# Where the maximum of quantised attention scores is joined, and who copies the transposed words

## The chip, the cores and the metric

The kernel runs on one core of a Trainium2 chip. The metric is the device time of one execution in microseconds; for the kernel before it is the median of three runs. A further execution was profiled, and everything that is read from views of the profile comes from that one. Five engines of the core appear: TensorE (PE, with its weight loads as PEld), VectorE (DVE), ScalarE (ACT), GpSimd (POOL) and SyncE (SP), which only issues transfers here. Each engine works through its own list of instructions in order, and semaphores make one engine wait for another.

## The reference

The reference is a two-layer decoder over 2048 rows of 256 values: sparse and local attention, cross attention and an FFN, then windowed attention, cross attention over image and text, and a mixture of experts, each followed by a layer norm. The change lies in the first cross attention. Its keys, queries and values are rounded to 8 bits, and so are the softmax weights, unsigned, row by row:

```python
attn = jnp.einsum('bhqd,bhkd->bhqk', q, k)
attn = jax.nn.softmax(attn.astype(jnp.float32), axis=-1)
attn = _fq_unsigned(attn, axis=-1)       # s = max(x) / 255; q = clip(round(x / s), 0, 255) * s
out = jnp.einsum('bhqk,bhkd->bhqd', attn, v)
```

There are 16 heads of 16 dimensions, and every query meets all 2048 keys. The largest weight of a row is exp(0) over the sum, so `round(x / s)` is the rounded value of exp(score - max + ln 255): the kernel needs, for each query and head, the maximum over 2048 scores before it can take the exponential.

## The kernel before

The joint stage computes this cross attention and, woven into it, the FFN that follows. Its work is cut into 128 steps: 8 pairs of row blocks (`gp`), 8 pairs of heads (`i`), and the two row blocks of a pair (`u`). One step handles 128 query rows and two heads (`hh`), that is two score rows of 2048 keys for each query. A step has two halves (`part`), and a half has two score blocks of 512 keys for both heads, so four blocks ("quarters") in a step. The loop at the end of the listing writes the order of every engine's instructions out by hand: `later` and `due` put small operations of the FFN, the query preparation and the layer norm into set half-steps.

What happens to one step, over several turns of the loop:

- TensorE computes a block of scores into PSUM (`scores`, L788). There are two such buffers (`s`).
- VectorE scales the block by the query's step and writes it to SBUF as `e` (`scaled`, L795). The same instruction puts the block's maximum into `smx`. In the kernel before, quarters 1 to 3 start from the maximum of the quarter before, which they read as a per-partition operand, so that the fourth column holds the maximum of the row so far. The first quarter has `None` there. In the profile each of these is TENSOR_SCALAR_CACHE_REDUCE with a DVE_READ_ACCUMULATOR behind it.
- ScalarE turns the maximum into ln 255 - max (`exponent`, L810, tile `snl`), at the end of the step.
- One turn later ScalarE takes the exponential of 2048 scores at a time to unsigned bytes (`weights8`, L819), once in each half.
- TensorE transposes these as words of four bytes (`words_T`, L831) into one of two PSUM buffers. The words are copied to SBUF (`words_out`, L837, tile `at`, three buffers): in the first half of a turn by VectorE, in the second by ScalarE.
- GpSimd spreads the bytes of the words to bfloat16 (`spread`, L841, tile `aT`), one cast of 2048 elements in each half.
- TensorE multiplies by the values (`context`, L854).

In a turn of the loop, VectorE's list holds the half's four scalings, then additions and other small work that is due, then the words of the first half. ScalarE's holds small copies that are due first, then the exponential, the words of the second half, the FFN's gate functions (L940, L941), and at the end of the second half `exponent`. GpSimd's holds the cast, then the FFN's elementwise work (L944, L947, L948), query rounding (L618 to L628) and norms; in the first 16 steps it also adds a bias to one row block a step (L1121). FFN work goes to eight of every 16 steps (`units`), from the second pair of row blocks on.

Of the kernel before, what the change touches and what calls it, by code (L numbers as in the profile page):

```python
# [18 lines left out]
F32 = mybir.dt.float32  # L19
# [3 lines left out]
AF = mybir.ActivationFunctionType  # L23
ALU = mybir.AluOpType
AX = mybir.AxisListType
PSUM = bass.MemoryType.PSUM

P = 128
# [20 lines left out]
def decoder(ctx: ExitStack, tc: tile.TileContext, w: dict, out: bass.AP):  # L49
    nc = tc.nc  # L50

    const = ctx.enter_context(tc.tile_pool(name="const", bufs=1))
    stat = ctx.enter_context(tc.tile_pool(name="stat", bufs=4))
# [156 lines left out]
    with ExitStack() as ph:  # L210
        pool = ph.enter_context(tc.tile_pool(name="l0a", bufs=1))
# [12 lines left out]
        wts, bias = {}, {}  # L224
# [297 lines left out]
        states, cks = {}, {}  # L522
# [66 lines left out]
    with ExitStack() as ph:  # L589
        pool = ph.enter_context(tc.tile_pool(name="l0x", bufs=1))  # L590
# [172 lines left out]
        nc.sync.dma_start(out=wp2, in_=w["L0_xattn_Wp"].rearrange("(c p) n -> p c n", p=P))  # L763
        for c in range(2):
            nc.gpsimd.tensor_scalar(wp2[:, c], wp2[:, c], sv[:, c : c + 1], 1.0, ALU.mult, ALU.mult)
        ln255 = pool.tile([P, 1], F32, name="ln255")
        nc.gpsimd.memset(ln255, math.log(255.0))

        wk = ph.enter_context(tc.tile_pool(name="l0x_k", bufs=2))
        ps = ph.enter_context(tc.tile_pool(name="l0x_ps", bufs=1, space=PSUM))  # L770
# [20 lines left out]
        def scaled(gp, i, u, half, c, st, s):  # L791

            quarter = 2 * half + c
            for hh in range(2):
                nc.vector.tensor_scalar(  # L795
                    st["e"][hh][:, half, c * G : (c + 1) * G],
                    s[:, hh, :],
                    qs[2 * gp + u][:, 2 * i + hh : 2 * i + hh + 1],
                    None if quarter == 0 else st["mx"][:, quarter - 1, hh : hh + 1],
                    ALU.mult,  # L800
                    ALU.max,
                    accum_out=st["mx"][:, quarter, hh : hh + 1],
                )
# [2 lines left out]
            return 4 * (i // 2) + i % 2 + 2 * hh  # L806

        def exponent(st):
            st["nm"] = stat.tile([P, 2], F32, tag="snl", name="snl")
            nc.scalar.activation(st["nm"], st["mx"][:, 3, :], AF.Identity, bias=ln255, scale=-1.0)  # L810

        def weights8(gp, i, u, hh, st):

# [20 lines left out]
        def words_out(hh, st, pt, copy):  # L834

            at = wk.tile([P, 4, P], F32, tag="at", name="at", bufs=3)
            copy(at.bitcast(U16), pt.bitcast(U16))  # L837
            st["at"][hh] = at
# [126 lines left out]
        states, aTs, os = {}, {}, {}  # L965
# [10 lines left out]
        def due(at, engine):  # L976
            for f, args in put_off.pop((at, engine), []):
                f(*args)
# [131 lines left out]
        states, aTs, os = {}, {}, {}  # L1110
# [3 lines left out]
        with tc.manual_schedule(engines=set(ordered)):  # L1114
            for n in range(len(steps) + 9):
                now = steps[n] if n < len(steps) else None
                if now is not None:
                    if n % 16 == 0:
                        group(n // 16)
                    if n < NB:  # L1120
                        nc.gpsimd.tensor_tensor(xs[n], xs[n], bp, ALU.add)  # L1121
                    states[n] = {
                        "e": [wk.tile([P, 2, 2 * G], F32, tag="e", name="e", bufs=4) for _ in range(2)],
                        "mx": stat.tile([P, 4, 2], F32, tag="smx", name="smx"),
                        "a": [],
                        "at": {},
                    }
                for part in range(2):
                    at = 2 * n + part
                    if now is not None:  # L1130
                        if at == 0:
                            waiting = scores(*now, 0, 0)
                        scaled(*now, part, 0, states[n], waiting)
                        scaled(*now, part, 1, states[n], scores(*now, part, 1))
                    due(at, "DVE")
                    m = n - 2 + part
                    due(at, "PE")
                    for hh in range(2):

                        q = n - 3 if (n - 3) % 2 == 1 else n - 4  # L1140
                        turn = (2 * (n - q) + part, hh)

                        if hh == 1 and 0 <= m < len(steps):
                            pt = words_T(1 - part, states[m])
                        if hh == 1 and at + 1 < 2 * len(steps):
                            waiting = scores(*steps[(at + 1) // 2], (at + 1) % 2, 0)
                        if 0 <= q < len(steps) and turn in turns:
                            gp, i, _ = steps[q]
                            if turn == (7, 0) and i % 4 == 0:
                                os[gp, i // 4] = ps.tile([P, 2 * P], F32, tag="o", name="o")  # L1150
                            o = os[gp, i // 4]
                            context(i, range(*turns[turn]), aTs[gp, i], o)
                            if turn == (9, 1):
                                aTs.pop((gp, i))
                                if i % 4 == 3:
                                    later(
                                        at + 1,
                                        "ACT first",
                                        nc.scalar.copy,
                                        ot[:, i // 4],  # L1160
                                        os.pop((gp, i // 4)).rearrange("p (u q) -> p u q", u=2),
                                    )
                                if i == 7 and gp < LAST:
                                    later(at, "DVE last", sums, gp)
                                    for u in range(2):
                                        later(at + 1, "POOL", by_dim, gp, u)
                    if part == 1:
                        unit(n, 1, at)
                    due(at, "ACT first")

                    if 0 <= n - 1 < len(steps):
                        weights8(*steps[n - 1], part, states[n - 1])
                    if 0 <= m < len(steps):
                        words_out(1 - part, states[m], pt, nc.scalar.copy if part else nc.vector.tensor_copy)
                    due(at, "ACT")
                    if 0 <= n - 2 < len(steps):
                        gp, i, u = steps[n - 2]
                        if part == 0 and u == 0:
                            aTs[gp, i] = wk.tile([P, NB, 2, 2 * P], BF16, tag="aT", name="aT")
                        due(at, "POOL first")  # L1180
                        spread(u, part, states[n - 2], aTs[gp, i])
                    due(at, "POOL first")
                    due(at, "POOL")
                    if now is not None and part == 1:
                        exponent(states[n])
                    due(at, "DVE last")
                    if (n, part) == (len(steps), 1):
                        later(at + 1, "DVE", sums, LAST)
                        for u in range(2):
                            later(at + 2, "POOL", by_dim, LAST, u)  # L1190
                    if n < len(steps):
                        pair_work(n, bool(part))
                    else:
                        tail_work(n, bool(part))
                if n == len(steps) + 3:
                    ffn_load_all()
                states.pop(n - 3, None)
            assert not put_off, put_off

            for i in range(NI):  # L1200
                for n in range(2):
                    ffn_gate(LAST, i, n, "s")
                th, gu = ffn_tiles(LAST, i, tail=True)
                ffn_out(LAST, th, gu)
                ffn_sigmoid(th, nc.vector)
                ffn_mult(LAST, i, th, gu, nc.vector)
            exp_tables()
            for u in range(2):
                ffn_put_out(LAST, range(NI * u, NI * u + NI), 0, "s")
                due(1, "DVE")  # L1210
            due(1, "POOL")
            due(2, "POOL first")
# [201 lines left out]
    with ExitStack() as ph:  # L1414
        pool = ph.enter_context(tc.tile_pool(name="l1a", bufs=1))
# [39 lines left out]
        with tc.manual_schedule(engines={mybir.EngineType.PE}):  # L1455
# [4 lines left out]
            for n in range(len(steps) + 16):  # L1460
# [3 lines left out]
                if n in (5, 7):  # L1464
                    q = NB // 2 - 2 + n // 7
# [132 lines left out]
    with ExitStack() as ph:  # L1598
# [29 lines left out]
        for g in range(NG):  # L1628
            parts = []
            for i in range(3):  # L1630
                at, rows = i * P, min(P, IS - i * P)
                wsh = moe_w["sh"]
                h = gated(g, rows, wsh[:, :, at : at + rows], wsh[:, :, IS + at : IS + at + rows])
                parts.append((h, moe_w["sd"][:rows, i, :], rows))
            for i in range(NI):
                at = slice(i * P, (i + 1) * P)
                h = gated(g, P, moe_w["g"][:, :, at], moe_w["u"][:, :, at], shares(g, i))
# [73 lines left out]
```

## Time and profile before

| | us |
|---|---|
| median of three runs (2859.89 to 2861.86) | 2860.21 |
| the profiled execution's own time | 2860.04 |
| its span, first to last instruction | 2858.3 |
| busy in the span: TensorE | 2607.9 |
| VectorE | 2071.4 |
| ScalarE | 1584.7 |
| GpSimd | 1238.4 |

A row of a group shows the line, the engine, the operation, what it writes and reads with shapes, how often it ran, then after the bar its busy time in us and the mean duration of one in ns, and after the second bar how long the engine was idle just before these instructions and what ended most of that. A duration runs from an instruction's start to its end; the next one on the same engine often starts a little before that end, so that the time from start to start is what an instruction costs its engine. A row of the timeline shows start (us), duration (us), engine, line and operation. A busy TensorE is not TensorE at its peak, because ends of matrix products are modelled, and some of their records are missing. Slices of the span are given in tenths of busy time, 9 meaning 90% or more.

### The profile page before, as it was taken

Reading aid. Unit: us, or ns where it says so; the run is one execution under the profiler, and the core shown is the slowest. Engines: PE = TensorE matmul, PEld = TensorE weight load, DVE = VectorE, ACT = ScalarE, POOL = GpSimd, SP = SyncE. Lnnn points to the kernel's source line nnn. Section 1 sums busy time; section 2 is a strip of 40 time slices with the busy share of each in tenths; the row PEclk is TensorE's granted clock in tenths of the full one; section 3 lists DMA queues with packets and bytes.
Section 4 is the critical chain, followed back from the end, with each engine's and each line's share of the span. In section 5 each row is a group of like instructions: output and inputs, shape, how many; then the busy total and the mean of one; then the engine's idle time right before and its main releaser. Section 6 shows DMA issues by size and latency. Waiting matters only on the chain. (4 is left out here: it accounts for less than half of the span.)

```text
span 2858.3 us, 44732 instructions
## 1 busy us (share of the span) xinstructions
PE 2607.9 (91%) x15989; PEld 1620.2 (57%) x16020; DVE 2071.4 (72%) x5525; ACT 1584.7 (55%) x2858; POOL 1238.4 (43%) x1390
## 2 busy tenths in 40 slices
PE   6999999999976788888889888899988899999998
PEld 3677777777753344444445444566655555665646
DVE  5677877877759999999999995577877763233232
ACT  3455555555536888878888885455555442222120
POOL 5644544444446667768777776323322200000000
PEclk9999999999996889999999999999999999999999
DMA  8000000000010000000000001400010012111120
GB/s 239 2 1 1 1 1 1 1 1 1 1 38 10 1 12 20 25 12 25 23 12 27 19 16 50 145 2 1 2 49 12 6 38 67 36 53 48 41 62 13
DMA packets 85006, 79.69 MB, mean 28 GB/s; under 512 B 19728, under 2 KB 66288, under 8 KB 84272
## 3 DMA queue, kind: packets, MB, share of 16 engines
q1 hardware_dynamic: 83520, 73.41, 8.5%
q0 software_dynamic: 1264, 3.42, 0.5%
q8 instruction: 127, 2.08, 0.3%
q14 instruction: 95, 0.78, 0.1%
HBM read 74.57 MB, written 2.23 MB: 27 GB/s over the span
## 5 line engine op out<-in xcount | busy, mean ns | idle before, releaser
L795 DVE TENSOR_SCALAR_CACHE_REDUCE e<-s,qs,smx 128x512 f32<-128x512 f32 x768 | 581.5, 806 | 12.3 <-PE s L788 11.7
L841 POOL CAST aT<-at 128x2048 bf16<-128x2048 uint8 x256 | 482.9, 1891 | 194.7 <-DVE at L837 133.4
L819 ACT ACTIVATE a<-e,snl 128x2048 uint8<-128x2048 f32 x256 | 510.8, 1998 | 2.8
L788 PE MATMUL s<-kT,qT 64*128 64x512 bf16 x1024 | 216.4, 416 | 99.6 <-DVE e L795 97.1
L1623 DVE TENSOR_TENSOR h<-h,up 128x512 f32<-128x512 f32 (+1 forms) x100 | 68.8, 688 | 192.6 <-PE up L1619 191.3
L854 PE MATMUL o<-aT,vq 128*32 128x256 bf16 x2048 | 193.7, 294 | 0.0
L831 PE MATMUL aTp<-ident,a 128*128 128x128 f32 x1024 | 181.7, 304 | 13.0 <-ACT a L819 12.6
L788 PEld LDWEIGHTS <-qT 64*128 64x128 bf16 x1024 | 61.9, 94 | 228.6 <-issue 227.5
L795 DVE TENSOR_SCALAR_CACHE_REDUCE e<-s,qs 128x512 f32<-128x512 f32 x256 | 179.6, 739 | 4.8 <-PE s L788 4.8
L1622 ACT ACTIVATE h<-gate 128x512 f32<-128x512 f32 (+1 forms) x100 | 59.7, 597 | 220.5 <-PE gate L1619 220.3
L1619 PE MATMUL gate<-xT,w_L_ffn_w1g 128*128 128x512 f32 x352 | 167.7, 595 | 0.0
L837 ACT COPY at<-aTp 128x1024 uint16<-128x1024 uint16 x128 | 128.4, 1003 | 69.6 <-PE aTp L831 64.7
L1619 PE MATMUL up<-xT,w_L_ffn_w1u 128*128 128x512 f32 x352 | 165.4, 592 | 0.0
L1333 DVE TENSOR_REDUCE amx<-sc 128x8 f32<-128x1024 f32 x96 | 116.7, 1215 | 62.2 <-PE sc L1324 62.0
L831 PEld LDWEIGHTS aTp<-ident,a 128*128 128x128 f32 x1024 | 116.6, 150 | 77.2 <-issue 35.8
L1650 PE MATMUL py<-w_L_ffn_w2T,h 128*128 128x256 f32 x704 | 154.6, 379 | 0.0
L1336 ACT ACTIVATE pr<-pr 128x1024 f32<-128x1024 f32 x96 | 101.6, 1059 | 88.3 <-DVE pr L1335 88.3
L1345 ACT COPY prT<-tp 128x512 f32<-128x512 f32 x192 | 104.2, 583 | 76.8 <-PE tp L1344 76.4
L1650 PEld LDWEIGHTS py<-w_L_ffn_w2T,h 128*128 128x128 f32 x704 | 133.7, 190 | 18.3
L922 PE MATMUL gu<-xT,wgu 128*128 128x256 f32 x448 | 128.4, 410 | 1.8 <-ACT gu_s L941 1.7
L854 PEld LDWEIGHTS <-vq 128*32 128x32 bf16 x2048 | 72.7, 98 | 100.0 <-issue 94.5
L443 ACT ACTIVATE pls<-sc,lm,rms_rs 128x128 f32<-128x128 f32 x256 | 113.7, 453 | 21.7 <-DVE lm L439 21.7
(319 smaller groups left out, 5961.7 us busy)
## 6 DMA issues: line engine op xcount, KB each, us to landing
wgu<-in_L_ffn_gu SPq DMA_DIRECT2D x112, 128.0 KB
sh<-share SPq DMA_DIRECT2D x32, 256.0 KB
sh<-share SPq DMA_DIRECT2D x16, 224.0 KB
sh<-share SPq DMA_DIRECT2D x16, 192.0 KB
w_L_ffn_w1g<-in_L_ffn_w1g SPq DMA_DIRECT2D x1, 2816.0 KB
w_L_ffn_w1u<-in_L_ffn_w1u SPq DMA_DIRECT2D x1, 2816.0 KB
w_L_ffn_w2T<-in_L_ffn_w2T SPq DMA_DIRECT2D x1, 2816.0 KB
sh<-share SPq DMA_DIRECT2D x16, 160.0 KB
```

What stands on the lines that cost most here:

```text
L443: nc.scalar.activation(pls[:, h, :], by_head[:, h // 2, h % 2, NC4:NK], AF.Exp, bias=nm[:, h : h + 1], scale=rq[:, h : h + 1], accum_out=s ...
L788: nc.tensor.matmul(s[:, hh, :], lhsT=qT[t % 4][r, i, :], rhs=kT[r, i, at : at + G], start=True, stop=True)
L795: nc.vector.tensor_scalar(st["e"][hh][:, half, c * G : (c + 1) * G], s[:, hh, :], qs[2 * gp + u][:, 2 * i + hh : 2 * i + hh + 1], None if ...
L819: nc.scalar.activation(a.bitcast(U8), st["e"][hh].rearrange("p a b -> p (a b)"), AF.Exp, bias=st["nm"][:, hh : hh + 1], accum_out=groups[g ...
L831: nc.tensor.transpose(pt[:, b, :], st["a"][hh][:, b * P : (b + 1) * P], ident)
L837: copy(at.bitcast(U16), pt.bitcast(U16))
L841: nc.gpsimd.tensor_copy(aT[:, :, hh, u * P : (u + 1) * P].rearrange("p (b j) q -> p b j q", j=4), st["at"].pop(hh).bitcast(U8).rearrange(" ...
L854: nc.tensor.matmul(o[r : r + 32], lhsT=vq[:, n, h // 2, h % 2 : h % 2 + 2].rearrange("p w d -> p (w d)"), rhs=aT[:, n, hh], start=n == 0 a ...
L922: nc.tensor.matmul(ffn_ps[q][:, n, :], lhsT=wt[:, k, :], rhs=xT[q // 2][:, k, at], start=k == 0, stop=k == 1)
L1333: nc.vector.tensor_reduce(mx, sc, AX.X, ALU.max)
L1619: nc.tensor.matmul(pp[:rows], lhsT=wt[:, k, :], rhs=xT[g][:, k, :], start=k == 0, stop=k == 1)
L1650: nc.tensor.matmul(py, lhsT=h[:rows, i4 * P : (i4 + 1) * P], rhs=wt, start=n == 0, stop=n == len(parts) - 1)
```

## The change

All of it is in the joint stage. First, `scaled` no longer passes the earlier maximum: each of the four quarters writes its own block's maximum. Second, `exponent` now joins the four columns by a reduction on VectorE and makes ln 255 - max on VectorE as well, with two constants; the constant tile `ln255` and ScalarE's operation go away. Third, `exponent` is issued right after the second half's scalings, and no longer at the end of the turn. Fourth, VectorE copies the words only where the half-step number is a multiple of four (first halves of even steps); ScalarE copies the other three of four.

```diff
-        ln255 = pool.tile([P, 1], F32, name="ln255")
-        nc.gpsimd.memset(ln255, math.log(255.0))
...
-                    None if quarter == 0 else st["mx"][:, quarter - 1, hh : hh + 1],
+                    None,
                     ALU.mult,
                     ALU.max,
                     accum_out=st["mx"][:, quarter, hh : hh + 1],
...
         def exponent(st):
+            m = stat.tile([P, 2], F32, tag="smm", name="smm")
+            nc.vector.tensor_reduce(m, st["mx"].rearrange("p q h -> p h q"), AX.X, ALU.max)
             st["nm"] = stat.tile([P, 2], F32, tag="snl", name="snl")
-            nc.scalar.activation(st["nm"], st["mx"][:, 3, :], AF.Identity, bias=ln255, scale=-1.0)
+            nc.vector.tensor_scalar(st["nm"], m, -1.0, math.log(255.0), ALU.mult, ALU.add)
...
                         scaled(*now, part, 1, states[n], scores(*now, part, 1))
+                        if part == 1:
+                            exponent(states[n])
                     due(at, "DVE")
...
-                        words_out(1 - part, states[m], pt, nc.scalar.copy if part else nc.vector.tensor_copy)
+                        words_out(1 - part, states[m], pt, nc.vector.tensor_copy if at % 4 == 0 else nc.scalar.copy)
...
-                    if now is not None and part == 1:
-                        exponent(states[n])
```

## The prediction

> **What bounds the kernel now.** I read the page's busy slices first (40 of 71.5 us), then the stretch in which the changed lines run, then its groups, then the timeline of VectorE.
>
> ```profile
> DVE  5677877877759999999999995577877763233232
> ACT  3455555555536888878888885455555442222120
> POOL 5644544444446667768777776323322200000000
> ```
>
> VectorE is at 9 tenths in slices 13 to 24 alone, and that is where the joint stage lies. It runs from VectorE's first scaling (879.6 us) to its last (1749.9 us). Columns of the stretch: TensorE, its weight loads, VectorE, ScalarE, GpSimd (instructions in brackets), granted clock.
>
> ```profile
> 879.60:1750.00 870.40, 740.25 (x4941) 392.33 (x4939) 854.77 (x2308) 732.10 (x909) 638.46 (x569) 0.91 0.06 17
> ```
>
> VectorE is busy 854.8 of 870.4 us: it sets the pace of all 128 steps. ScalarE has 138 us free, GpSimd 232 us. The groups of the stretch:
>
> ```profile
> L795 DVE TENSOR_SCALAR_CACHE_REDUCE e<-s,qs,smx 128x512 f32<-128x512 f32 x768 | 581.5, 806 | 12.3 <-PE s L788 11.7
> L795 DVE TENSOR_SCALAR_CACHE_REDUCE e<-s,qs 128x512 f32<-128x512 f32 x256 | 179.6, 739 | 4.8 <-PE s L788 4.8
> L837 ACT COPY at<-aTp 128x1024 uint16<-128x1024 uint16 x127 | 127.4, 1003 | 69.6 <-PE aTp L831 64.7 <-POOL aT L841 4.7
> L837 DVE COPY at<-aTp 128x1024 uint16<-128x1024 uint16 x126 | 86.2, 684 | 0.0
> L810 ACT ACTIVATE snl<-smx,ln 128x2 f32<-128x2 f32 x127 | 38.5, 303 | 33.3 <-DVE e L795 33.2
> L841 POOL CAST aT<-at 128x2048 bf16<-128x2048 uint8 x252 | 475.4, 1891 | 194.5 <-DVE at L837 133.4 <-ACT at L837 57.7 <-PE o L854 1.9
> ```
>
> The same scaling takes 806 ns where it reads the running maximum and 739 ns where it does not. Mean durations overlap, so the cost is read from start to start on VectorE's timeline:
>
> ```profile
> 1310.69 0.74 DVE L795 TENSOR_SCALAR_CACHE_REDUCE e<-s,qs 128x512 f32<-128x512 f32 x1
> 1311.36 0.74 DVE L795 TENSOR_SCALAR_CACHE_REDUCE e<-s,qs 128x512 f32<-128x512 f32 x1
> 1312.03 0.80 DVE L795 TENSOR_SCALAR_CACHE_REDUCE e<-s,qs,smx 128x512 f32<-128x512 f32 x1
> 1312.77 0.80 DVE L795 TENSOR_SCALAR_CACHE_REDUCE e<-s,qs,smx 128x512 f32<-128x512 f32 x1
> 1313.50 0.68 DVE L837 COPY at<-aTp 128x1024 uint16<-128x1024 uint16 x1
> 1314.10 0.80 DVE L795 TENSOR_SCALAR_CACHE_REDUCE e<-s,qs,smx 128x512 f32<-128x512 f32 x1
> ```
>
> 0.67 us without the operand, 0.733 with it, 0.60 for the copy (the accumulator read behind each scaling lies under the next instruction). A step is 6 x 0.733 + 2 x 0.67 + 0.60 = 6.34 us, and from 1310.69 to 1317.03 it is just that. A step in which something else were the bound would be longer.
>
> **Taken from VectorE.** (1) The pointer operand of 768 scalings: 768 x 0.063 = 48.4 us. (2) Half of its word copies: 64 x 0.602 = 38.5 us. Together 86.9 us, or 0.68 us a step; all of it is on the path, since VectorE is.
>
> **Put on VectorE.** Two tiny instructions a step, each needing the one before. No row has this pair, but a chain like it is at 309.48: a 0.29 us reduction of 128 elements, then a dependent operation of 0.17 us starting 0.03 after its end. Here: wait out the last accumulator read (0.07), 0.03, reduce 8 elements (0.17), 0.03, scale 2 elements (0.16), less 0.08 by which the next instruction overlaps: 0.39 us. Bounds: 0.30 if both overlap their neighbours fully (2 x 0.15), 0.50 if neither does. At 0.39: 128 x 0.39 = 49.9 us. Behind the pair are queued the block additions due in that half-step and the next step's eight scalings; TensorE waits for those to free its two score buffers, and ScalarE's exponentials wait for the pair's result.
>
> **The port, which speaks against the change.** VectorE's new scale reads and writes SBUF in fp32 with two constants. Rows of this form before (L469, and L665 with 128x2) show this:
>
> ```profile
> 51.63 0.72 POOL L388 TENSOR_TENSOR raw_Wlk<-raw_Wlk,gains 128x256 f32<-128x256 f32 x1 [0.47 <-ACT sq L384]
> 51.66 0.72 DVE L469 TENSOR_SCALAR sums<-sums 128x8 f32<-128x8 f32 x1
> ...
> 69.86 0.17 DVE L469 TENSOR_SCALAR sums<-sums 128x8 f32<-128x8 f32 x1
> ...
> 835.99 0.62 POOL L716 TENSOR_TENSOR ka<-ka,kr 128x256 f32<-128x256 f32 x1
> 836.17 0.47 DVE L665 TENSOR_SCALAR sv<-sv 128x2 f32<-128x2 f32 x1
> ```
>
> With GpSimd idle it takes 0.17 us; with GpSimd in an instruction it ends 0.03 us after that instruction does (52.38 against 52.35; 836.64 against 836.61). The Trainium skill, page "SBUF — State Buffer", section "Who interferes with whom", says why: VectorE and GpSimd share one pair of SBUF ports, a tensor_scalar that can use both ports takes the pair, and the second to ask is fully blocked until the first is done. The scaling at L795 writes an accumulator and reads PSUM, so it is spared; ScalarE, where the value is made now, never waits for that pair. By the 0.17 us row alone the change is worth 86.9 - 49.9 = **37.0 us faster**; by the rule each step also waits for the rest of GpSimd's instruction, which in this stage is mostly a 1.89 us cast. No row shows a cast blocking VectorE; I take it to do what the additions do.
>
> How long is the wait? If the scale came at random: 252 casts x 1.891² / (2 x 870.4) = 0.52 us, some 0.05 more for the smaller instructions, 0.57. Placed where VectorE's steps end in this trace (0.95 us after the start of the last scaling), what was left of GpSimd's instruction averages 0.78. Both ends use phases that the change moves, so I place them by hand. Steps of even number keep VectorE's copy (8 x 0.67 + 0.60 + 0.39 = 6.35 us), odd ones lose it (5.75); the scale is ready 0.08 before the end.
> - Even, no FFN work: VectorE's copy ends at 3.3, cast one runs 3.4 to 5.3; ScalarE's copy of the other half waits for TensorE's transposes and ends near 5.2, so cast two runs 5.3 to 7.2. The scale, ready at 6.27, waits 0.9, and the step is some 0.8 longer.
> - Odd, no FFN work: ScalarE now has both copies; its exponentials and copies (0.18 + 1.99 + 0.89 + 1.99 + 1.0) end at 6.05, and cast two starts then. The scale at 5.67 finds GpSimd free: 0. Mean 0.40.
> - The first 16 steps: GpSimd has an addition of 0.72 (L1121) between the casts, so cast two runs 6.0 to 7.9 in even steps: 1.55, mean 0.78.
> - FFN steps (56): GpSimd also has 0.41 + 0.73 + 0.73 us. Even: the last product (L948) runs to about 6.75, so 0.4 longer; odd: between 0 and 0.7, as ScalarE lags by 1.0 to 1.6. Mean 0.35.
> Sum: 16 x 0.78 + 56 x 0.40 + 56 x 0.35 = 54.5 us, or 0.43 a step.
>
> **ScalarE.** It loses 127 small operations (29 us net of overlap) and gains 64 copies (64 x 0.946 = 60.5): 732 + 31 = 763 us, under VectorE's 855 - 37. In an FFN pair of steps it has 6.51 (odd: 2 x 1.99 + 2 x 0.89 + 0.28 + 0.47) and 5.62, together 12.13, against VectorE's 6.35 + 5.75 = 12.10 without waits: level. TensorE has 11.6 there (8 x 0.33 scores, 4 x 0.59 transposes, 32 x 0.074 contexts, 4 x 1.07 FFN, from start to start). So without port waits a few tenths a pair would be lost (28 x 0.28 = 8 us); with them ScalarE has room again and costs nothing. Its new copy sits behind the first exponential, which ends 2.2 us into a step, while the transposes are done by 1.9: no new wait for TensorE. If that cover went, 0.3 us in 64 steps. The removed constant is one memset ahead of the stage: nothing. The moved step issues no DMA and passes no queue of SyncE or GpSimd.
>
> **Sum.** -86.9 + 49.9 + 54.5 = +17.5 us on the profiled execution's 2860.04 (2858.3 of span, 1.7 around it): 2877.5. The median of the runs is 2860.21, so 2878. The point that decides: a port wait of 0.68 - 0.39 = **0.29 us a step**.
>
> **Rivals.** (A) The forecast, 62%. (B) Faster, 20%: the pair rarely meets a busy GpSimd, or a cast does not hold the ports. 2860 - 37 + 8 = 2831. For it: GpSimd is idle a quarter of the stage and which quarter that is hangs on copies that the change moves. Against it: L665 and L469. (C) Much slower, 10%: phases stay as they are, 128 x 0.78 = 100, so 2860 - 37 + 100 = 2923; against it, half of the copies that release casts move. (D) ScalarE becomes the bound, 8%: if steps can't lend each other time, an FFN pair is 6.51 + 6.35 = 12.86 against 12.68 now (+5 us on 28 pairs), while the other 36 pairs gain 0.58 (-21): 2844, or, with some port waits, no change. Against it: the e tiles are double-buffered by step, with 0.3 to 2.5 us spare in FFN steps now.
>
> **Chances.** About 0.2% (6 us) is what a measurement tells from no change. B gives 20% faster, D is split between faster and the same, A and C are slower but for a few per cent of A that land within 6 us: 0.23, 0.08, 0.69. The range takes in all but the bottom of B and the top of C: 2830 to 2915. A alone, with the pair at 0.30 to 0.50 (-12, +14 us) and the wait at 0.30 to 0.57 (-16, +18), spans 2858 to 2901 when these are added in squares.
>
> **What would show it.** L795 as one group of 1024 at 740 ns; the word copies 64 on VectorE and 192 on ScalarE; the new scale at a mean of 0.5 to 0.7 us rather than 0.17, with its longest near 2 us, ending with a GpSimd cast; steps of 5.75 and 7.1 us in turn. A scale at 0.17 throughout would make it wrong in sign, and a scale near 1 us would make it too mild.

## The result, and the profile after

The changed kernel takes 2897.23 us (median of 4 runs, 2893.65 to 2903.64) against 2860.05 for the kernel before (median of 4 as well): 1.0135 times as long, 95% interval 1.0118 to 1.0152, or 37 us more. Slower was forecast, and the time lies in the range of 2830 to 2915, but 17.5 us had been worked out and 37 came.

The joint stage, from VectorE's first scaling to the end of its last, grew from 870.4 to 908.0 us; what follows it takes 1108.4 us in both. The stretch of the stage in the changed kernel, with the columns of the prediction, the last three being the granted clock of TensorE, the share of the DMA engines and GB/s:

```profile
879.56:1787.54 907.98, 746.80 (x4936) 394.68 (x4934) 870.33 (x2499) 755.60 (x845) 636.26 (x568) 0.91 0.06 16
```

VectorE is busy for 870.3 us (854.8 before), and it stands idle for 37.7 us (15.6 before). So 15.6 of the stage's 37.6 us are more work or blocking, and 22.0 are more standing still. The granted clock is 0.91 in both stages. The groups of the same stretch:

```profile
L793 DVE TENSOR_SCALAR_CACHE_REDUCE e<-s,qs 128x512 f32<-128x512 f32 x1024 | 704.9, 743 | 30.3 <-PE s L786 28.8
L841 POOL CAST aT<-at 128x2048 bf16<-128x2048 uint8 x252 | 475.1, 1891 | 222.2 <-ACT at L837 196.5 <-DVE at L837 19.1 <-PE s L786 3.0
L837 ACT COPY at<-aTp 128x1024 uint16<-128x1024 uint16 x190 | 192.6, 1014 | 60.4 <-PE aTp L831 58.9 <-POOL aT L841 1.1
L810 DVE TENSOR_SCALAR snl<-smm 128x2 f32<-128x2 f32 x128 | 78.2, 611 | 4.5
L837 DVE COPY at<-aTp 128x1024 uint16<-128x1024 uint16 x63 | 43.2, 685 | 0.0
L808 DVE TENSOR_REDUCE smm<-smx 128x2 f32<-128x8 f32 x128 | 20.6, 161 | 4.4
```

The scaling is one group of 1024 at 743 ns, as forecast. The new scale of two elements (L810) averages 0.611 us. Unblocked it is 0.17, so 78.2 - 128 x 0.17 = 56.4 us of it are waiting; 54.5 had been put down. The last column of L793 is what had not: VectorE waits 30.3 us ahead of its scalings, 28.8 of them for TensorE's scores, where the two groups of before add up to 17.1. The timeline has both at one place:

```profile
1360.20 1.89 POOL L841 CAST aT<-at 128x2048 bf16<-128x2048 uint8 x1 [0.60 <-ACT at L837]
1360.28 1.83 DVE L810 TENSOR_SCALAR snl<-smm 128x2 f32<-128x2 f32 x1
1362.03 0.41 DVE L890 TENSOR_TENSOR x<-x,pd 128x256 f32<-128x256 f32 x1
1362.49 2.93 PE L957 MATMUL pd<-w_L_ffn_d,h 128*128 128x256 f32 x6 [2.70 <-DVE x L890]
1365.35 0.61 PE L786 MATMUL s<-kT,qT 64*128 64x512 bf16 x2
1366.00 0.75 DVE L793 TENSOR_SCALAR_CACHE_REDUCE e<-s,qs 128x512 f32<-128x512 f32 x1 [1.53 <-PE s L786]
```

GpSimd's cast runs from 1360.20 to 1362.09, and the scale that comes at 1360.28 ends at 1362.11. The addition queued behind it is late, TensorE waits 2.70 us for that, its six products then take 2.93 us, and the scores behind them make VectorE wait 1.53 us more. The same six products in the trace of before, and the changed kernel's clock (third column from the end) here and at the same place one block of 16 steps later:

```profile
1343.06 1.56 PE L957 MATMUL pd<-w_L_ffn_d,h 128*128 128x256 f32 x6 [0.97 <-DVE x L890]
...
1362.49:1365.42 2.93, 2.93 (x8) 1.92 (x8) 1.94 (x6) 1.76 (x2) 0.00 (x0) 0.50 0.00 0
1479.61:1481.17 1.56, 1.56 (x8) 1.12 (x8) 1.53 (x5) 1.56 (x1) 0.00 (x0) 1.00 0.00 0
```

TensorE stands for 2.69 to 2.70 us at six such places. At three of them the granted clock is then 0.50, the six products take 2.93 us and VectorE waits behind them; at the other three it is 1.00, they take 1.56 us and VectorE does not wait behind them. So the port wait alone does not make the second wait of this example; the half clock is in it too. Why it comes at three of the six, no run shows.

### The profile page after: what moved, and what is told of

The parts are those of the page before. It is cut to its first block, busy times and chain, and to the rows that moved or that the text cites. A ratio compares the mean times of both kernels' runs of the same rounds, so it can differ in the third digit from the quotient of the medians.

```text
span 2895.9 us, 44578 instructions
## 1 busy us (share of the span) xinstructions
PE 2618.0 (90%) x16020; PEld 1622.9 (56%) x16020; DVE 2086.5 (72%) x5717; ACT 1609.3 (56%) x2794; POOL 1236.6 (43%) x1389
## 3 DMA queue, kind: packets, MB, share of 16 engines
q8 instruction: 127, 2.08, 0.3%
## 5 line engine op out<-in xcount | busy, mean ns | idle before, releaser
L793 DVE TENSOR_SCALAR_CACHE_REDUCE e<-s,qs 128x512 f32<-128x512 f32 x1024 | 704.9, 743 | 30.3 <-PE s L786 28.8
L837 ACT COPY at<-aTp 128x1024 uint16<-128x1024 uint16 x192 | 194.7, 1014 | 60.4 <-PE aTp L831 58.9
L831 PE MATMUL aTp<-ident,a 128*128 128x128 f32 x1024 | 183.3, 306 | 14.9 <-ACT a L819 13.9
L373 PE MATMUL proj<-Wlk,xT 128*128 128x512 f32 x256 | 121.3, 596 | 3.4 <-DVE ck L341 1.2
```

What stands on the lines that cost most here:

```text
L793: nc.vector.tensor_scalar(st["e"][hh][:, half, c * G : (c + 1) * G], s[:, hh, :], qs[2 * gp + u][:, 2 * i + hh : 2 * i + hh + 1], None, AL ...
L831: nc.tensor.transpose(pt[:, b, :], st["a"][hh][:, b * P : (b + 1) * P], ident)
```

## The experiments

Two accounts of the missing 20 us were open. By the first, the port waits cost more than their own length, since they hold up TensorE as above. By the second, the copies that ScalarE took over do not give VectorE's time back. Five runs separate port and copies; the runs after that look into the copies. The kernel before was run again beside each group of runs (medians 2858.15 to 2860.60), and each ratio below is to the one beside it.

**Without the port.** Two reductions in place of a reduction and a scale:

```diff
-            m = stat.tile([P, 2], F32, tag="smm", name="smm")
-            nc.vector.tensor_reduce(m, st["mx"].rearrange("p q h -> p h q"), AX.X, ALU.max)
+            m = joins[st["n"] % 4]        # [P, 2, 2], filled with ln 255 once
+            nc.vector.tensor_reduce(m[:, :, 0], st["mx"].rearrange("p q h -> p h q"), AX.X, ALU.max, negate=True)
             st["nm"] = stat.tile([P, 2], F32, tag="snl", name="snl")
-            nc.vector.tensor_scalar(st["nm"], m, -1.0, math.log(255.0), ALU.mult, ALU.add)
+            nc.vector.tensor_reduce(st["nm"], m, AX.X, ALU.add)
```

> The changed kernel, but ln 255 - max is made by two reductions (a negated maximum beside a constant ln 255, then their sum) and no longer by a scale with two constants: as many small VectorE operations in the same place, none of which takes the port pair. Port theory: the 56 us of waits in the scale vanish, and with them the 12 us in which VectorE then stood before TensorE's scores; the pair keeps its own 0.41 us a step. 2897 - 56 - 12 = 2829, 2822 to 2838, each small operation near 0.16 us with none over 0.3. Rival (ScalarE's third copy in four costs the part that the forecast lacked): the 56 us go but 15 to 20 us stay, 2840 to 2850. Rival (a dependent tiny pair is slow in itself): 2885 to 2900.

Measured: 2849.0 us, 0.9959 of the kernel before (0.9944 to 0.9974). The stage of this kernel, and its second reduction (shortest, median and longest, in ns):

```profile
879.07:1737.70 858.63, 725.24 (x4936) 385.74 (x4934) 816.72 (x2499) 753.21 (x843) 634.92 (x567) 0.94 0.06 17
...
L814 DVE TENSOR_REDUCE snl<-join x128: 156/157/158, 884.8 to 1738.0; 128x2 f32<-128x4 f32 x128
```

The waiting is gone from the small operation, which keeps to 0.158 us at most, and 48 us are gained. VectorE's busy time, 816.7 us, is 38.1 under that of before, as the prediction had it without the port (37.0). But the stage is only 11.7 us shorter: VectorE now stands idle for 41.9 us. The rival for ScalarE, 2840 to 2850, has the time of this run; that the port waits carried TensorE's delays with them, 2822 to 2838, does not.

**Shorter casts.** The port claim from the other side: the changed kernel with each cast in two.

```diff
-            nc.gpsimd.tensor_copy(
-                aT[:, :, hh, u * P : (u + 1) * P].rearrange("p (b j) q -> p b j q", j=4),
-                st["at"].pop(hh).bitcast(U8).rearrange("p b (q j) -> p b j q", j=4),
-            )
+            dst = aT[:, :, hh, u * P : (u + 1) * P].rearrange("p (b j) q -> p b j q", j=4)
+            src = st["at"].pop(hh).bitcast(U8).rearrange("p b (q j) -> p b j q", j=4)
+            for b in (slice(0, 2), slice(2, 4)):
+                nc.gpsimd.tensor_copy(dst[:, b], src[:, b])
```

> The changed kernel with each GpSimd cast of 2048 elements cut into two of 1024. Port theory: a wait lasts until the instruction in hand ends, so its longest falls from 1.9 to about 1.0 us and the 51 us that were waited on casts fall by about half; with the waits for scores that follow them 20 to 35 us are gained: 2862 to 2877. Rival (the scale waits for something else that happens to end then): no change, 2890 to 2902, longest scale still 1.9 us.

Measured: 2886.14 us, 1.0093 of before (1.0076 to 1.0110). The cast and the scale:

```profile
L844 POOL CAST aT<-at x512: 1032/1042/1051, 891.0 to 1784.0; 128x1024 bf16<-128x1024 uint8 x171
...
L810 DVE TENSOR_SCALAR snl<-smm x128: 169/357/1049, 885.2 to 1773.0; 128x2 f32<-128x2 f32 x128
```

The longest scale is now 1.049 us, where it was 1.901, and the longest cast 1.051: at both lengths VectorE waits for the instruction in hand. The gain, 11 us, is half of the least expected, and the time lies between the two ranges. Two halves take 2.08 us where one cast took 1.89, and scales longer than 0.25 us became more frequent (85 of 128, from 70), so the waits fell from 56.4 to 41.2 us only.

**The join alone, and the copies alone.** First the changed kernel with the copies as before, then the kernel before with the copies changed:

```diff
-words_out(1 - part, states[m], pt, nc.vector.tensor_copy if at % 4 == 0 else nc.scalar.copy)
+words_out(1 - part, states[m], pt, nc.scalar.copy if part else nc.vector.tensor_copy)
```

> The changed kernel with the word copies as before, half on VectorE and half on ScalarE: only the maximum part of the change. Port theory: VectorE loses 44 us of operand time and gains 52 us for the pair, and every step now has the long phase in which a cast is running when the scale comes (0.4 to 0.9 us a step, 50 to 115 us): 2920 to 2985, slower than the full change. Rival (ScalarE's load is what the forecast lacked): about 2897 + 38 - 20 = 2915 or less.

> The kernel before with only the copies changed (ScalarE makes three of four). No scale on VectorE, so no port wait. VectorE gives up 38 us. ScalarE keeps its small operation and has 12.9 us in a pair of FFN steps against VectorE's 12.1, so part comes back there: 28 pairs x 0.8 = 22 at most. 2822 to 2844, faster than before. Rival (the copies themselves cost the missing part): 2850 to 2865.

Measured: the join alone 2918.87 us, 1.0205 of before (1.0190 to 1.0220), 1 us under the range of the port account and 4 over the rival's; the copies alone 2865.68 us, 1.0020 of before (1.0012 to 1.0028), where 2822 to 2844 was expected and the rival said 2850 to 2865. Handing 64 copies to ScalarE takes 38 us from VectorE (64 x 0.602) and makes the kernel 5 us slower. Of the join alone, the scalings, and of the copies alone, the stage and the scalings:

```profile
L793 DVE TENSOR_SCALAR_CACHE_REDUCE e<-s,qs 128x512 f32<-128x512 f32 x1024 | 706.1, 742 | 14.9 <-PE s L786 14.3
```

```profile
879.23:1748.40 869.17, 728.68 (x4936) 386.75 (x4934) 823.17 (x2244) 783.96 (x970) 636.40 (x567) 0.93 0.06 17
...
L795 DVE TENSOR_SCALAR_CACHE_REDUCE e<-s,qs,smx 128x512 f32<-128x512 f32 x768 | 579.7, 808 | 23.8 <-PE s L788 22.4
L795 DVE TENSOR_SCALAR_CACHE_REDUCE e<-s,qs 128x512 f32<-128x512 f32 x256 | 181.5, 741 | 23.7 <-PE s L788 14.7 <-ACT a L819 8.0
```

With all the port waits but the old copies, VectorE waits 14.9 us ahead of its scalings, less than the 17.1 of before. With the new copies and no port wait at all it waits 47.5. So the added waits come with the copies. The waits in the scale itself are nearly the same with and without the moved copies, 56.4 and 55.5 us, so what the copies bring beside the port waits is not a change in those waits.

**The fourth corner.** Two reductions, copies as before (the edits of the first run and of the third together).

> The join by two reductions (no port) with the copies as before: the fourth corner of port and copies, beside 2849 (no port, copies moved), 2919 (port, copies as before) and 2897 (port, copies moved). VectorE's own account is -44 to -48 for the operand and +50 to +53 for the pair, 2860 to 2869 with nothing else. If the port wait is the whole difference, this is 50 to 58 us under 2919: 2861 to 2869. If ScalarE's exponentials, which now wait for VectorE's pair, add a wait of their own, above 2872.

Measured: 2860.54 us, 1.0010 of before (1.0003 to 1.0017), at the bottom of what VectorE's own account gave. VectorE's pair costs what the operand saves, to 2 us, and no cost of the longer way from VectorE to ScalarE's exponential shows in the time. In the four corners, by the medians:

| | copies as before | ScalarE copies three of four | worth of the copies |
|---|---|---|---|
| two reductions, no port | 2860.5 | 2849.0 | -11.5 |
| a reduction and a scale | 2918.9 | 2897.2 | -21.7 |
| worth of the port | +58.4 | +48.2 | |

By the ratios, which take out the difference between the groups of runs, the copies are worth -14.6 and -20.0 us and the port +55.8 and +50.3: the differences of two kernels are uncertain by some 3 us.

**What the copies run into.** In the copies-only kernel, ScalarE's first exponential is cut to half in the turns of odd steps with FFN work, which leaves out half of the weights there:

```diff
-                a.bitcast(U8),
-                st["e"][hh].rearrange("p a b -> p (a b)"),
+                a.bitcast(U8)[:, 0 : 2 * G] if short else a.bitcast(U8),
+                st["e"][hh][:, 0, :] if short else st["e"][hh].rearrange("p a b -> p (a b)"),
...
-weights8(*steps[n - 1], part, states[n - 1])
+weights8(*steps[n - 1], part, states[n - 1], part == 0 and n % 2 == 1 and busy(n))
```

> The copies-only kernel, in which ScalarE's first exponential of 28 odd FFN steps takes 1024 of its 2048 scores and leaves the other half of the words stale: 0.85 us less for ScalarE in just the steps where it has the added copy of 0.89. VectorE, TensorE and GpSimd keep their work. Theory (ScalarE's load in FFN steps holds up the others): the waits of VectorE fall from 42 us to 13 to 20, and 20 to 30 us are gained against 2866: 2836 to 2846. Rival (the place of the copy in ScalarE's list, or TensorE itself, is the limit): 2858 to 2868.

Measured: 2845.37 us, 0.9958 of before (0.9943 to 0.9972): 20.3 us under the copies-only kernel, or 18 by the ratios, for 27 x 0.85 = 23.0 us less of ScalarE's work (the trace has 27 short exponentials, not 28), while VectorE's list is the same. The time is within what was expected, but the waits ahead of VectorE's scalings fell only from 47.5 to 33.2 us, not to 13 to 20. What ScalarE no longer has to do there comes back nearly whole; yet the copies-only kernel had lost 38 + 5 = 43 us, so this is less than half of the loss. The kernel before with the short exponentials was not run, so that they gain only beside the moved copies is not shown.

Then the opposite, the kernel before with copies moved only in the 30 odd steps with neither FFN gates nor query work:

```diff
-words_out(1 - part, states[m], pt, nc.scalar.copy if part else nc.vector.tensor_copy)
+words_out(1 - part, states[m], pt, nc.scalar.copy if part or quiet(n) else nc.vector.tensor_copy)
```

> The kernel before, in which ScalarE takes VectorE's word copy only in the 30 odd steps that have no FFN work and no query work beside them. VectorE gives up 30 x 0.602 = 18 us. Theory (ScalarE has no room in FFN steps, and its lateness reaches VectorE through TensorE's scores): the 30 copies in quiet steps cost nothing, so the whole 18 us are gained although fewer copies move than in the copies-only kernel: 2842, 2837 to 2848. Rival (a copy on ScalarE comes late wherever it is): as the copies-only kernel in proportion, 2857 to 2866.

Measured: 2851.06 us, 0.9976 of before (0.9967 to 0.9985). Some thirty copies (29 in the trace) gain 7 us where sixty-four lose 5, so where they are moved decides. But 18 us were expected. Read off the timelines, the first 16 steps give only 3.3 us, four of their odd steps the full 0.6. Counted from 0 in a later block of 16, and as means of five such blocks, step 5 takes 7.78 us as before, and what step 3 gives (6.60 to 6.14) step 4 takes back (7.31 to 7.77). In steps 3 to 5 TensorE has the FFN's second product (L957): quiet for ScalarE, but not for TensorE.

**The scale on ScalarE.** The changed kernel, with the join on VectorE and ln 255 - max on ScalarE at the old place; first with the copies as before, then with all of the moved copies, then with the 30 of the quiet steps:

```diff
+        def joined(st):        # where exponent(st) is in the changed kernel
+            st["m"] = stat.tile([P, 2], F32, tag="smm", name="smm")
+            nc.vector.tensor_reduce(st["m"], st["mx"].rearrange("p q h -> p h q"), AX.X, ALU.max)
...
-            nc.vector.tensor_scalar(st["nm"], m, -1.0, math.log(255.0), ALU.mult, ALU.add)
+            nc.scalar.activation(st["nm"], st["m"], AF.Identity, bias=ln255, scale=-1.0)
```

> The changed kernel with the copies as before and ln 255 - max made on ScalarE at the end of the turn, as before; only the maximum over the four columns is on VectorE. VectorE loses 44 to 48 us of operand time and gains one reduction, 0.23 us a step, 29 us; nothing takes the port pair and ScalarE has what it had: 2860 - 17 = 2843, 2838 to 2850. If the scale's port wait were not what made the join alone slow (2919), it would be near 2885 or above.

> The join on VectorE with ln 255 - max on ScalarE, and ScalarE making three of four copies in all steps. By VectorE's work alone 38 us less than 2839.5 (the same with the copies as before): 2801. Theory (no room on ScalarE in FFN steps, nor on TensorE where the FFN's second product runs): the 34 copies in the other steps take back more than they give, so slower than 2827 with 30 copies moved: 2838 to 2852.

> The two together: four independent maxima joined by one reduction on VectorE, ln 255 - max on ScalarE, and ScalarE's third copy only in the 30 quiet odd steps. If the parts add up, 2860 - 17 - 18 = 2825, 2818 to 2834, faster than both kernels.

Measured: 2839.47 us (0.9938 of before, 0.9922 to 0.9955), 2852.81 (0.9983, 0.9975 to 0.9991) and 2827.43 (0.9896, 0.9881 to 0.9911). The first and the last are within what was expected; the second is 1 us slower than its range. The last is 31 us under the kernel before that ran beside it and, by the ratios, 68 under the changed one. The scalings with all copies moved, and of the last kernel the stage and the scalings:

```profile
L796 DVE TENSOR_SCALAR_CACHE_REDUCE e<-s,qs 128x512 f32<-128x512 f32 x1024 | 708.9, 744 | 57.9 <-PE s L789 48.1 <-ACT a L824 7.1 <-PE pt_r L881 0.3
```

```profile
881.05:1715.10 834.05, 713.48 (x4938) 381.74 (x4936) 813.50 (x2406) 754.02 (x938) 637.50 (x568) 0.95 0.06 18
...
L796 DVE TENSOR_SCALAR_CACHE_REDUCE e<-s,qs 128x512 f32<-128x512 f32 x1024 | 706.2, 744 | 17.5 <-PE s L789 15.9 <-issue 0.3
```

The waits ahead of the scalings follow the copies in all kernels: 13.0 to 17.1 us with the copies as before, whatever makes the maximum; 17.5 and 22.1 with those of the quiet steps moved; 30.0 to 34.5 with 64 moved and the small operation off ScalarE; 47.5 and 57.9 with 64 moved and the small operation still on it (33.2 with the short exponentials).

## Why the prediction was right or wrong, point by point

**Right: the bound, the operand and the pair.** VectorE is the busiest engine of the stage before and after, though it does not set the pace of all 128 steps: already before it waited 17.1 us ahead of its scalings. Scalings start every 0.67 us, so 48.4 us of operand are gone as worked out. An unblocked odd step lasts 5.77 to 5.79 us in the first 16, that is 8 x 0.67 and 0.41 to 0.43 for the pair (forecast 0.39; its terms add up to 0.38): some 53 us, 3 more than the 49.9. With the copies as before and no port wait, operand and pair cancel to 2 us in the time.

**Right: the port.** The scale that meets a cast ends 0.02 us after it (median). The wait, the point said to decide, was put at 0.43 us a step and is 0.44. Removing it brings 48 us, or 58 with the old copies. That a cast holds the port as GpSimd's additions do had been an inference; 59 scales end with a cast and have 48.1 us of the waiting, and the other 8.4 us end with GpSimd's tensor_tensor instructions. That the sum fits so well is in part luck: 0.51 a step in the first 16 (0.78 forecast) and 0.29 in FFN steps (0.35) are offset by 0.56 in the others (0.40).

**Wrong: what the copies give back.** The step that failed is the 38.5 us of word copies counted in full as saved, by "all of it is on the path, since VectorE is" and "with them ScalarE has room again and costs nothing". VectorE gave up the copies, but only 21.7 us of that arrive in the time (2918.9 to 2897.2): 17 of the missing 20 us. In the trace it is 13.2 us more of waiting ahead of the scalings than before. With the 17.5 us worked out, 3 more for the pair and 2 for the port, that makes some 36 of the stage's 37.6 us; it is an estimate, since it mixes costs from start to start with idle times.

Where VectorE stands idle can be read off the timelines by kinds of steps, with the steps counted as above:

| more idle time of VectorE, us | join alone to changed kernel (port waits in both) | two reductions, copies as before to moved | before to copies alone |
|---|---|---|---|
| FFN steps (ScalarE has gate functions) | 4.6 | 9.3 | 19.0 |
| steps 3 to 5 of the later blocks (TensorE has L957) | 9.7 | 5.5 | 7.4 |
| step 13 of the later blocks (query work) | -0.2 | 4.4 | 4.1 |
| all 128 steps | 15.2 | 21.2 | 30.4 |

So the FFN steps, where the working looks for ScalarE's room, have the largest part only without port waits. With port waits they have 4.6 us: not nothing, but little. The largest part in the changed kernel is in the steps of the FFN's second product. TensorE's sum in the working (11.6) is for FFN steps alone, and these other steps were left out. At full clock VectorE waits 0.54 us behind the last eight of those products with the join and the copies as before, and 1.14 with the copies moved as well, with port waits or without; half clock at three places makes some 2 us of the 9.7. That two score buffers are too few to carry work from one step into the next is my reading of the waits; no run had a third buffer.

The 8 us that the level sums (12.13 against 12.10) were to cost without port waits were too mild as well: the loss was 26 us there (38.1 less work, 11.7 less time).

**Rivals.** B, faster at 2831, named the right case without the port, but its time was 2849 for the same reason. D, ScalarE as the bound, had 8% as an alternative to the port; without the port waits the FFN steps have the largest part of the idle time, and with them a smaller one than TensorE's steps. A loss of this kind beside A was the case that the forecast lacked.

**Left open.** The copies-only kernel's stage is 1.1 us shorter than before, yet the kernel takes 5 us more; its trace has 5.5 us more behind the last scaling, of which the later end of the last cast explains 1.5. Which part of the copies' loss is TensorE's and which ScalarE's was only bounded, in the copies-only kernel: of some 43 us, 18 to 20 went with 23.0 us of ScalarE's work. For the changed kernel the table above says where VectorE stands, not what alone would end it. The granted clock of the stage goes from 0.90 (join alone) to 0.95 (the last kernel), and no run holds it fixed; the copies-only kernel has 0.93 against 0.91 before and is the slower one, so it does not order the times.

## What to carry to other kernels

Before a tiny operation is moved to VectorE, look what else of its form did while GpSimd was busy: two elements waited for a whole cast, and two reductions or ScalarE did the same job without. When work leaves the engine that sets the pace, count the gain step by step against every other engine in the same step, not against idle sums over the stage; where one of them is full, the gain turns into waits. Here moving 29 copies gained more than moving 64.

## What the runs showed of the hardware that was not expected

A VectorE instruction on two elements per partition was held for up to 1.90 us by one GpSimd cast, and for up to 1.05 us when the cast was cut in two. A cut cast costs 2 x 1.042 us against 1.891. After TensorE had stood for 2.69 to 2.70 us, the granted clock was 0.50 at three places of six, and fp32 products of 256 columns took 0.634 to 0.795 us each there, where 0.379 is their median.
